# Half of the relu to VectorE, five more gathered columns to ScalarE, one register load for two chunks on SyncE

## The chip, the cores and the metric

One Trainium2 chip, of which the program uses one core. The metric is the device time of the whole program in microseconds. The kernel before takes 3349.78 us (median of 3 runs, 3347.76 to 3354.19). The engines are called as in the profile: PE is TensorE (PEld its weight loads), DVE is VectorE, ACT is ScalarE, POOL is GpSimd, SP is SyncE; a trailing q means the sequencer of that engine.

## The reference

One message-passing layer of a graph network: 12,500 nodes of 48 features, 400,000 edges with 32 features each, sorted by destination.

```python
h   = maximum(layernorm(x), 0)                       # 12500 x 48
tmp = concatenate([h[dst], h[src], edge_attr], 1)    # 400000 x 128
e   = relu(tmp @ W1 + b1)                            # 400000 x 128
msg = e @ W2 + b2                                    # 400000 x 48
out = x + segment_sum(msg, dst, 12500)
```

## The kernel before

The product with `W1` is split by its inputs. Two tables are made once: table A is `h @ W1[:48] + b1` and table B is `h @ W1[48:96]`, both 12,544 rows of 128 floats in the chip's memory; B is also kept transposed in SBUF (`bt`, one column of 128 values for each node). The edges are then taken in 391 chunks of 8 tiles of 128 edges. For a tile, `pre` in PSUM is the sum of a matmul that spreads the few rows of table A that the chunk needs and adds the edge features (`before`, line 409), and of the rows of table B that belong to the tile's source nodes (`gathered`, line 430). `hidden` (line 446) is the relu of the whole chunk out of PSUM, by ScalarE. `fold` (line 456) multiplies by a 0/1 matrix `hot` to sum over equal destinations, `add` (line 471) adds the result into a window `seg` of SBUF, and every 12 to 44 chunks (103 for the first) a full window is multiplied by `W2`, added to x and stored.

Source rows reach a tile in one of three ways, and the tiles are dealt out so that all engines have a share:

- **POOL**: an indirect DMA for each tile, 128 rows of table B into `gb` (line 379). `gb` has 8 buffers, one for each chunk.
- **Columns**: VectorE and ScalarE copy single columns out of `bt` into `gt` (line 352). A register holds the place of each column; `numbers` (line 276) loads a group of registers at once. `PARTS` lists eleven groups for each chunk with their places and sizes: five of VectorE (8, 15, 16, 20, 12: 71 columns) and six of ScalarE (12, 8, 8, 20, 12, 12: 72 columns). 143 columns for each chunk make one whole tile in every 128/143 of a chunk; `BYCOLS` deals these tiles out over chunks 5 to 389.
- **Rows**: SP sends 15 DMAs of one row for each chunk into `gs` (line 293), by registers that it has loaded with the start row of table A (line 369).

The schedule is written by hand (`manual_schedule`): each engine runs its instructions in the order of the program text. In turn `c` of the loop, chunk `c` is prepared (`prepare`: SP loads `lhs`, `row`, the registers and `rhs`, POOL gathers, VectorE makes the 0/1 matrix `lhs` at line 387), chunk `c-1` goes through `before`, `gathered` and `hidden`, and chunk `c-2` through `fold` and `add`. VectorE's order in a turn is `lhs`, columns 8 and 15, `add`, columns 16, `hot` (line 398), columns 20, columns 12. ScalarE's is columns 12, 8, 8, `hidden`, columns 20, 12, 12. PE's is `before`, `fold`, `gathered`. `pre`, `hot` and `p_g` have two buffers, `lhs`, `rhs`, `row` and `hid` three.

Of the kernel before, what the change touches and what calls it, by code (L numbers as in the profile page):

```python
# [8 lines left out]
F32 = mybir.dt.float32  # L9
I32 = mybir.dt.int32  # L10
AF = mybir.ActivationFunctionType
# [5 lines left out]
P = 128  # L17
N, D, DE, HID, E = 12500, 48, 32, 128, 400000
# [4 lines left out]
T = 8  # L23
CE = T * P
NCH = (NT + T - 1) // T
# [29 lines left out]
ROWS0 = 3  # L55
# [2 lines left out]

PARTS = (
    (True, 0, 8), (True, 8, 15), (True, 24, 16), (True, 40, 20), (True, 60, 12),  # L60
    (False, 72, 12), (False, 84, 8), (False, 92, 8), (False, 100, 20), (False, 120, 12),
    (False, 132, 12),
)
PLACE = 23
STRIP = 144
PART = sum(n for _, _, n in PARTS)
SLOT = [at + k for _, at, n in PARTS for k in range(n)]
FIRST_OF = [sum(n for _, _, n in PARTS[:k]) for k in range(len(PARTS))]
RPART = 15
BASE = 0  # L70

BT0 = 16512
SEG0 = 165792
SEG_SIZE = 8 * L


AT_PLACE, AT_SEG, SEG, NEXT = 16, 17, 18, 19
WIDTH = 20
SLOTS = (NCH + 2 + P - 1) // P
BANK = 4  # L80

# [147 lines left out]
def windows(nc, tc, gp, bt, ident, idx, raw, rhss, x_t, tab_a, tab_b, dst, edge_t, w2s, b2s,  # L229
# [5 lines left out]
    with ExitStack() as es:  # L235
# [26 lines left out]
        st = {}  # L262
        gts = {}
        gss = {}

        def group(c):

# [6 lines left out]
        def numbers(c, at, n, engine, table=last):  # L274

            return nc.values_load_multi_w_load_instructions(  # L276
                table[c % P : c % P + 1, c // P, at : at + n],
                engines=[engine], min_val=0, max_val=1 << 23,
                skip_runtime_bounds_check_because="numbers of nodes, and what is made of them",
            )[1]  # L280
# [77 lines left out]
        def prepare(c):  # L358
            n, w = min(T, NT - c * T), span(c)
            at = c * CE  # L360
            lhs = lhss[c % 3]
            nc.sync.dma_start(lhs[W:K, : n * P], edge_t[:, at : at + n * P])
            row = ld.tile([W, CE], I16, name="row")
            nc.sync.dma_start(
                row[:w, : n * P],
                dst[at : at + n * P].rearrange("(o e) -> o e", o=1).to_broadcast([w, n * P]),
            )
            m = max(0, min(RPART, len(BYROWS) * P - (c - ROWS0) * RPART)) if c >= ROWS0 else 0
            base, *nodes = numbers(c, BASE, 1 + m, mybir.EngineType.SP)
            rhs = rhss[c % 3]  # L370
            base = base.with_bounds(min_val=0, max_val=4 * HID * (N - 1))
            nc.sync.dma_start(
                rhs.bitcast(U8)[:w, :],
                taba8[bass.ds(base, 4 * HID * w)].rearrange("(w h) -> w h", w=w),
            )
            st[c] = dict(n=n, rows=nodes)
            gb = gp.tile([P, T, HID], F32, name="gb") if c >= RAW else None
            for t in range(n - len(COLS_OF.get(c, ())) - (c in BYROWS) if c >= RAW else 0):
                nc.gpsimd.indirect_dma_start(  # L379
                    out=gb[:, t, :], out_offset=None, in_=tab_b[:, :],  # L380
                    in_offset=bass.IndirectOffsetOnAxis(
                        ap=srci[:, c * T + t : c * T + t + 1], axis=0
                    ),
                )

            deg = degs[c % 3]
            nc.vector.tensor_scalar(  # L387
                lhs[:w, : n * P], row[:w, : n * P], bw[:w, c : c + 1], None,
                op0=ALU.is_equal, op1=ALU.add, accum_out=deg[:w, :1],
            )  # L390
            st[c].update(rhs=rhs, lhs=lhs, gb=gb, deg=deg)
# [23 lines left out]
        def gathered(c):  # L415

            s = st[c]
            if c < RAW:
                for q in range(T // 2):
                    nc.tensor.matmul(  # L420
                        s["pre"][:, 2 * q : 2 * q + 2, :], s["hx"][:, q, :], wb,
                        start=False, stop=True, skip_group_check=True,
                    )
                return
            pre, js = s["pre"], COLS_OF.get(c, ())
            m = s["n"] - len(js)
            g = m - (c in BYROWS)

            def add(lhsT, rhs, t, e):
                nc.tensor.matmul(  # L430
                    pre[:, t:e, :], lhsT, rhs, start=False, stop=True, skip_group_check=True
                )

            for t, j in enumerate(js, m):
                add(gts.pop(j), ident, t, t + 1)
            if g < m:
                add(ident, gss.pop(c), g, m)
            for t in range(0, g, BANK):
                e = min(g, t + BANK)
                add(ident, s["gb"][:, t:e, :], t, e)  # L440

        def hidden(c):
            s = st[c]
            n = s["n"]
            h = wp.tile([P, T, HID], F32, name="hid")
            nc.scalar.activation(h[:, :n, :], s["pre"][:, :n, :], AF.Relu)  # L446
            s["h"] = h

        def fold(c):
            s = st[c]  # L450
# [61 lines left out]
        with tc.manual_schedule():  # L512
            for c in range(NCH + 2):
                g, k = group(c - 2)
                if c < NCH:
                    prepare(c)
                    rows(c, st[c].pop("rows"))
                if 0 <= c - 1 < NCH:
                    before(c - 1)
                if 0 <= c - 2 < NCH:  # L520
                    fold(c - 2)
                columns(c, 0)
                columns(c, 1)
                segment_add()
                if 0 <= c - 2 < NCH:
                    add(c - 2)
                    if c - 1 == begin(g + 1) < NCH:
                        segment_next(g)
                columns(c, 2)
                if c < NCH:  # L530
                    compare(c)
                if c < 2:
                    nc.vector.memset(segs[c], 0.0)
                columns(c, 3)
                columns(c, 4)
                columns(c, 5)
                columns(c, 6)
                columns(c, 7)
                if 0 <= c - 1 < NCH:
                    gathered(c - 1)  # L540
                    hidden(c - 1)
                columns(c, 8)
                columns(c, 9)
                columns(c, 10)
                if c + 1 == begin(g + 1) or c == NCH - 1:
                    segment_load(g)
                if g > 0 and k < L // BLK:
                    segment_sum(g - 1, k, BLK)
                if g > 0 and k == (STORE if begin(g + 1) < NCH else 2):
                    segment_store(g - 1, L)  # L550
                if c == NCH + 1:
                    segment_sum(g, 0, END_L)
                    segment_add()
                    segment_store(g, END_L)
                if c < RAW:
                    raw_turn(c)
                if c == 1:
                    sources()
                for i in range(c * TURNS, min((c + 1) * TURNS, BLOCKS)):
                    turn(i)  # L560

                if c < PIECES:
                    s = slice(c * PIECE, (c + 1) * PIECE)
                    nc.sync.dma_start(out_t[:, s], x_t[:, s])
# [126 lines left out]
def tile_gnn_preln(  # L691
# [71 lines left out]
    with tc.tile_pool(name="keep", bufs=1) as keep, tc.tile_pool(  # L763
# [82 lines left out]
        def check():  # L846

            p_c = ps_c.tile([1, P], F32, name="p_c")
            nc.tensor.transpose(p_c, furthest, ident)
            out_of = keep.tile([1, 1], F32, name="out_of")  # L850
            nc.vector.tensor_reduce(out_of, p_c, AX.X, ALU.max)
            nc.vector.tensor_scalar(flag, out_of, 0.5, None, op0=ALU.is_gt)

            nc.vector.tensor_scalar(bw, b0f[:W, :], wcol[:W, :], None, op0=ALU.add)

            nc.vector.tensor_scalar(cols, cols, 4, BT0, op0=ALU.mult, op1=ALU.add)
            rows_at = slice(BASE, BASE + 1 + RPART)
            nc.vector.tensor_scalar(
                last[:, :, rows_at], last[:, :, rows_at], 4 * HID, None, op0=ALU.mult
            )  # L860
            nc.vector.tensor_tensor(
                last[:, :, NEXT : NEXT + 1], last[:, :, NEXT : NEXT + 1],
                last[:, :, SEG : SEG + 1], op=ALU.subtract,
            )
            at = last[:, :, AT_PLACE : AT_PLACE + 1]
            nc.vector.scalar_tensor_tensor(
                at, last[:, :, AT_SEG : AT_SEG + 1], -4.0, at, op0=ALU.mult, op1=ALU.add
            )
            at_place = slice(PLACE, PLACE + 1)
            nc.vector.scalar_tensor_tensor(  # L870
                cols[:, :, at_place], cols[:, :, at_place], 1.0, at, op0=ALU.mult, op1=ALU.add
            )
# [87 lines left out]
```

## Time and profile before

| | |
|---|---|
| median of 3 runs | 3349.78 us (3347.76 to 3354.19) |
| the profiled execution | 3348.55 us, of which the span on the core is 3346.8 us |
| granted TensorE clock | 0.875 |
| busy: PE, DVE, ACT, POOL | 84%, 78%, 91%, 75% |
| chunks, and first to last start of the DVE's `lhs` | 391, from 78.3 to 3328.5 us |
| indirect gathers of POOL at line 379 | 2618 |
| column copies of ACT and of DVE | 27705 and 27335 |

Busy time counts an engine's own instructions. Register loads, waits and the issue of DMAs are run by the engine's sequencer and count as idle, so an engine with a busy share of 78% may still have no time left. In a group's row, "idle before" is the idle time in front of its instructions and what ended it; "issue" there is time in which nothing that the profile shows was waited for, only the engine's own sequencer.

### The profile page before, as it was taken

How to read it: one execution, taken by the hardware profiler on the slowest of the kernel's cores; microseconds unless marked ns; L12 is line 12 of the kernel's file. 1: busy time of each engine (PE TensorE's matmuls, PEld its weight loads, DVE VectorE, ACT ScalarE, POOL GpSimd, SP SyncE). 2: the span in 40 equal slices, each digit the busy share in tenths (PEclk: the TensorE clock that was granted, in tenths of full speed). 3: DMA queues.
4: the chain of work that ended last, by engine and by line, in shares of the span. 5: the costliest groups of instructions: out<-in, count | busy, mean ns of one | idle time of the engine just before them, and what ended most of it. 6: DMA issues, size and time to landing. Idle time of an engine off the chain costs nothing.

```text
span 3346.8 us, 114800 instructions
## 1 busy us (share of the span) xinstructions
PE 2804.1 (84%) x16242; PEld 2228.4 (67%) x16242; DVE 2608.9 (78%) x29052; ACT 3044.9 (91%) x28183; POOL 2516.1 (75%) x2672
## 2 busy tenths in 40 slices
PE   7988888888888888888888888888877888788877
PEld 6676767666666676766666676666665666666655
DVE  6477777777777777788777777887878788888886
ACT  5799999999999998999999999999999999999997
POOL 7777777777777777777777777777777777777776
PEclk9988888888888888888888888998989888899898
DMA  7322223233333333333333333333333333333332
GB/s 259 110 77 78 77 77 78 76 80 83 84 83 82 83 82 83 84 89 88 86 86 88 87 88 85 93 91 93 93 93 93 93 90 93 96 100 98 100 98 76
DMA packets 171145, 307.66 MB, mean 92 GB/s; under 512 B 68611, under 2 KB 93813, under 8 KB 169093
## 3 DMA queue, kind: packets, MB, share of 16 engines
q0 software_dynamic: 84800, 172.53, 20.7%
q1 hardware_dynamic: 85170, 127.53, 12.7%
q14 instruction: 634, 5.19, 0.5%
q8 instruction: 137, 2.24, 0.3%
q10 hardware_dynamic: 404, 0.17, 0.0%
HBM read 284.21 MB, written 18.34 MB: 90 GB/s over the span
## 4 chain that ended last, share of the span: by engine, by line
DVE 34%; POOL 25%; issue 22%; PE 10%; ACT 4%; DMA 3%; DVEq 2%; ACTq 0%; SPq 0%; POOLq 0%
POOL gb L379 25%; DVE gt L352 25%; DVE lhs L387 6%; ACT gt L352 3%; DMA gb<-tab_b,srci 3%; PE pre L409 3%; PE pre L430 2%; PE p_g L456 2%; DVE hot L398 2%; DVEq L276 2%; PE p_n L194 1%; ACT hid L446 1%; DVE seg L471 1%; PE pre L306 0%; ACTq L276 0%
## 5 line engine op out<-in xcount | busy, mean ns | idle before, releaser
L379 POOL DMA_INDIRECT gb<-tab_b,srci x2618 | 2476.4, 946 | 805.3 <-issue 759.8
L352 ACT COPY gt<-bt 128x1 f32 x27705 | 2619.5, 188 | 76.6 <-issue 66.1
L352 DVE COPY gt<-bt 128x1 f32 x27335 | 1839.8, 143 | 616.7 <-issue 578.7
L430 PE MATMUL pre<-gb,ident 128*128 128x512 f32 (+2 forms) x1548 | 851.7, 668 | 234.9 <-DMA gb<-tab_b,srci 227.7
L409 PEld LDWEIGHTS pre<-rhs,lhs 112*128 112x128 f32 x6250 | 888.6, 220 | 187.0 <-issue 118.4
L409 PE MATMUL pre<-rhs,lhs 112*128 112x128 f32 x6250 | 884.3, 302 | 27.5 <-issue 17.1
L456 PE MATMUL p_g<-hot,hid 128*128 128x64 f32 (+4 forms) x6250 | 789.9, 279 | 111.2 <-ACT hid L446 109.2
L456 PEld LDWEIGHTS p_g<-hot,hid 128*128 128x128 f32 x6250 | 769.0, 200 | 139.7 <-ACT hid L446 138.8
L430 PEld LDWEIGHTS pre<-gb,ident 128*128 128x128 f32 x1548 | 314.3, 234 | 536.1 <-issue 469.0
L446 ACT ACTIVATE hid<-pre 128x1024 f32<-128x1024 f32 x391 | 397.7, 1017 | 175.4 <-PE pre L430 158.5
L387 DVE TENSOR_SCALAR_CACHE_REDUCE lhs<-row,bw 64x1024 f32<-64x1024 int16 (+4 forms) x391 | 492.2, 1259 | 3.0 <-DMA row<-in_dst 3.0
L430 PE MATMUL pre<-ident,gt 128*128 128x128 f32 x860 | 224.2, 349 | 137.9 <-DVE gt L352 118.8
L430 PEld LDWEIGHTS pre<-ident,gt 128*128 128x128 f32 x860 | 148.6, 217 | 157.6 <-issue 77.6
L398 DVE TENSOR_TENSOR hot<-wnum,rel 128x512 f32<-128x512 f32 (+4 forms) x391 | 207.0, 529 | 0.0
L459 PE MATMUL p_g<-ident,deg 80*128 80x32 f32 (+4 forms) x782 | 159.7, 286 | 0.0
L471 DVE TENSOR_TENSOR seg<-seg,p_g 128x128 f32 (+4 forms) x391 | 94.1, 241 | 80.6 <-PE p_g L459 79.9
L459 PEld LDWEIGHTS p_g<-ident,deg 80*128 80x128 f32 x782 | 128.3, 206 | 0.0
L499 PE MATMUL p_f<-seg,w2s 128*48 128x512 f32 (+1 forms) x58 | 35.9, 705 | 5.5 <-DVE xseg L506 5.1
L773 POOL DMA_INDIRECT xg<-in_x,srci x32 | 31.0, 967 | 10.2 <-issue 8.8
L500 PE MATMUL p_f<-seg,b2s 1*48 1x512 f32 (+1 forms) x58 | 33.3, 656 | 0.0
L203 ACT COPY tab<-p_n 128x512 f32<-128x512 f32 x33 | 18.7, 584 | 12.1 <-PE p_n L194 11.8
L387 DVE DVE_READ_ACCUMULATOR lhs<-row,bw 64x1 f32 (+4 forms) x391 | 28.8, 74 | 0.0
(78 smaller groups left out, 357.7 us busy)
## 6 DMA issues: line engine op xcount, KB each, us to landing
gs<-tab_b SPq DMA_DIRECT2D x5760, 0.5 KB
lhs<-in_edge_t SPq DMA_DIRECT2D x390, 128.0 KB
gb<-tab_b,srci POOLq DMA_INDIRECT x2618
row<-in_dst SPq DMA_DIRECT2D x90, 128.0 KB
row<-in_dst SPq DMA_DIRECT2D x85, 96.0 KB
row<-in_dst SPq DMA_DIRECT2D x50, 160.0 KB
row<-in_dst SPq DMA_DIRECT2D x87, 64.0 KB
tab_b<-tab SPq DMA_DIRECT2D x3, 1280.0 KB
```

What stands on the lines that cost most here:

```text
L276: return nc.values_load_multi_w_load_instructions(table[c % P : c % P + 1, c // P, at : at + n], engines=[engine], min_val=0, max_val=1 << 23,
L352: copy(gts[j][:, e : e + 1], bt8[:, bass.ds(of, 4)].bitcast(F32))
L379: nc.gpsimd.indirect_dma_start(out=gb[:, t, :], out_offset=None, in_=tab_b[:, :], in_offset=bass.IndirectOffsetOnAxis(ap=srci[:, c * T + t ...
L387: nc.vector.tensor_scalar(lhs[:w, : n * P], row[:w, : n * P], bw[:w, c : c + 1], None, op0=ALU.is_equal, op1=ALU.add, accum_out=deg[:w, :1],)
L398: nc.vector.tensor_tensor(hot[:, :n, :], wnum[:, :w].unsqueeze(1).to_broadcast([P, n, w]), rel[:, c * T : c * T + n].unsqueeze(2).to_broad ...
L409: nc.tensor.matmul(pre[:, t, :], s["lhs"][:K, t * P : (t + 1) * P], s["rhs"][:K, :], start=t % BANK == 0, stop=False, skip_group_check=True,)
L430: nc.tensor.matmul(pre[:, t:e, :], lhsT, rhs, start=False, stop=True, skip_group_check=True)
L446: nc.scalar.activation(h[:, :n, :], s["pre"][:, :n, :], AF.Relu)
L456: nc.tensor.matmul(p_g[:, 0, :], s["h"][:, t, :], s["hot"][:, t, :], start=t == 0, stop=t == n - 1)
L459: nc.tensor.matmul(p_g[:, 1, :], s["deg"], ident[:W, :w], start=True, stop=True)
L471: nc.vector.tensor_add(to, to, s["p_g"])
L499: nc.tensor.matmul(p_f[:, :n], w2s, seg[:, 0, s], start=True, stop=False)
```

## The change

- `prepare` loads SP's registers for two chunks in every even chunk: 2 x 15 rows and 2 starts, 32 numbers, in place of 16 in every chunk. The table of numbers is laid out anew for that.
- The relu of a chunk is split. `hidden_first` lets VectorE do tiles 0 to 3 with a `tensor_scalar_max`, and `hidden` leaves tiles 4 to 7 to ScalarE. `gathered` and `hidden_first` stand between VectorE's columns 20 and columns 12; ScalarE's part keeps its place behind its third group.
- ScalarE's groups of columns become 12, 8, 12, 20, 12, 13: 77 columns where there were 72. VectorE's 71 stay. With 148 columns for each chunk, more tiles come from columns and fewer from POOL.

```diff
 PARTS = (
     (True, 0, 8), (True, 8, 15), (True, 24, 16), (True, 40, 20), (True, 60, 12),
-    (False, 72, 12), (False, 84, 8), (False, 92, 8), (False, 100, 20), (False, 120, 12),
-    (False, 132, 12),
+    (False, 72, 12), (False, 84, 8), (False, 92, 12), (False, 104, 20), (False, 124, 12),
+    (False, 136, 13),
 )
+SHARE = 4
-STRIP = 144
+STRIP = 152
 RPART = 15
-BASE = 0
+BASE = 2 * RPART
...
+        ahead = []
...
-            base, *nodes = numbers(c, BASE, 1 + m, mybir.EngineType.SP)
+            if c % 2 == 0:
+                ahead[:] = numbers(c, 0, 2 * RPART + 2, mybir.EngineType.SP)
+            base, nodes = ahead[BASE + c % 2], ahead[c % 2 * RPART :][:m]
...
+        def hidden_first(c):
+
+            s = st[c]
+            s["h"] = wp.tile([P, T, HID], F32, name="hid")
+            nc.vector.tensor_scalar_max(s["h"][:, :SHARE, :], s["pre"][:, :SHARE, :], 0.0)
+
         def hidden(c):
             s = st[c]
-            n = s["n"]
-            h = wp.tile([P, T, HID], F32, name="hid")
-            nc.scalar.activation(h[:, :n, :], s["pre"][:, :n, :], AF.Relu)
-            s["h"] = h
+            of = slice(SHARE, s["n"])
+            nc.scalar.activation(s["h"][:, of, :], s["pre"][:, of, :], AF.Relu)
...
                 columns(c, 3)
+                if 0 <= c - 1 < NCH:
+                    gathered(c - 1)
+                    hidden_first(c - 1)
                 columns(c, 4)
                 columns(c, 5)
                 columns(c, 6)
                 columns(c, 7)
                 if 0 <= c - 1 < NCH:
-                    gathered(c - 1)
                     hidden(c - 1)
...
```

The rest of the diff lays the numbers out for two chunks on the host and moves the constants that go with it.

More of the change, by code (lines that the diff above doesn't have):

```diff
@@ L69 @@
 RPART = 15
-BASE = 0
+BASE = 2 * RPART
 BT0 = 16512
-SEG0 = 165792
+SEG0 = 166176
 SEG_SIZE = 8 * L
-AT_PLACE, AT_SEG, SEG, NEXT = 16, 17, 18, 19
-WIDTH = 20
+AT_PLACE, AT_SEG, SEG, NEXT = 32, 33, 34, 35
+WIDTH = 36
 SLOTS = (NCH + 2 + P - 1) // P
@@ L856, in check @@
             nc.vector.tensor_scalar(cols, cols, 4, BT0, op0=ALU.mult, op1=ALU.add)
-            rows_at = slice(BASE, BASE + 1 + RPART)
+            rows_at = slice(0, BASE + 2)
             nc.vector.tensor_scalar(
@@ L908 @@
     numbers[2 : NCH + 2, AT_PLACE] = SEG0 + of % 2 * SEG_SIZE - BT0
-    numbers[:NCH, BASE] = first
+    bases = np.pad(first, (0, -NCH % 2)).reshape(-1, 2)
+    numbers[: NCH + NCH % 2 : 2, BASE : BASE + 2] = bases
     numbers[:NCH, SEG] = seg
@@ L920 @@
     rows = by_tile[in_rows].reshape(-1)
-    rows = np.pad(rows, (0, -len(rows) % RPART)).reshape(-1, RPART)
-    numbers[ROWS0 : ROWS0 + len(rows), BASE + 1 : BASE + 1 + RPART] = rows
+    by_chunk = np.zeros((NCH + NCH % 2) * RPART, np.int32)
+    by_chunk[ROWS0 * RPART : ROWS0 * RPART + len(rows)] = rows
+    numbers[: NCH + NCH % 2 : 2, : 2 * RPART] = by_chunk.reshape(-1, 2 * RPART)
     last = np.ascontiguousarray(numbers.reshape(SLOTS, P, WIDTH).transpose(1, 0, 2))
```

## The prediction

> **What bounds the kernel now.** I read the busy shares first, then the costliest groups, then for each engine whether anything outside it ever stops it, and last one turn of VectorE in the timeline. From the page, part 1 and part 5:
>
> ```profile
> PE 2804.1 (84%) x16242; PEld 2228.4 (67%) x16242; DVE 2608.9 (78%) x29052; ACT 3044.9 (91%) x28183; POOL 2516.1 (75%) x2672
> ...
> L379 POOL DMA_INDIRECT gb<-tab_b,srci x2618 | 2476.4, 946 | 805.3 <-issue 759.8
> L352 ACT COPY gt<-bt 128x1 f32 x27705 | 2619.5, 188 | 76.6 <-issue 66.1
> L352 DVE COPY gt<-bt 128x1 f32 x27335 | 1839.8, 143 | 616.7 <-issue 578.7
> ```
>
> By busy time ScalarE looks like the bound and VectorE and POOL like engines with room. The idle columns say otherwise: of POOL's 805.3 us idle, 759.8 are its own issue, and of VectorE's 616.7 in front of its copies 578.7 are issue too, the sequencer fetching registers. So both are nearly full. For POOL, the timeline at the beginning, at its one long stop, and at the end:
>
> ```profile
> 52.58 0.94 POOL L379 DMA_INDIRECT gb<-tab_b,srci  x1 [1.77 <-issue]
> 53.83 0.95 POOL L379 DMA_INDIRECT gb<-tab_b,srci  x1 [0.30 <-issue]
> ...
> 128.07 0.94 POOL L379 DMA_INDIRECT gb<-tab_b,srci  x1 [5.88 <-PE pre L430]
> ...
> 3331.58 0.94 POOL L379 DMA_INDIRECT gb<-tab_b,srci  x1 [0.30 <-issue]
> ```
>
> A gather takes 1.25 us from start to start (53.83 - 52.58), and 2618 x 1.25 = 3273 us fill the 3279 us from 52.58 to 3331.58 but for the one stop of 5.88 us. POOL therefore sets today's end. But VectorE stands just behind it. Its waits in the windows 75 to 400, 400 to 1200, 1200 to 3300 and 3300 to the end, and the count of its `lhs` instructions (two records for each chunk) by stretch:
>
> ```profile
> DVE seg L471 <- PE p_g L459: 27.5, 4, 10.5
> ...
> DVE gt L352 <- issue: 169.5, 320, 1.1
> ...
> DVE gt L352 <- issue: 342.9, 789, 1.1
> DVE seg L471 <- PE p_g L459: 41.0, 24, 4.0
> ...
> DVE seg L471 <- PE p_g L459: 11.4, 4, 4.4
> ...
> 400.00:800.00 400.00, 62.58 (x100) 0.86 0.30 78
> 800.00:1200.00 400.00, 62.04 (x98) 0.85 0.32 83
> ...
> 2400.00:2800.00 400.00, 60.95 (x96) 0.90 0.35 92
> 2800.00:3200.00 400.00, 59.84 (x94) 0.90 0.37 98
> ```
>
> Between 400 and 1200 us VectorE waits for no other engine at all; 198 records are 99 chunks in 800 us, 8.08 us for each. There VectorE sets the pace, and POOL, which began early, lives on its eight buffers of lead. Between 2400 and 3200 the pace is 8.42 us (190 records, 95 chunks) and VectorE now and then waits for PE, which waits for POOL. Over the whole stretch from 1200 to 3300 those waits are only 41.0 us. So VectorE could take about 41 us more, 0.1 us for each of 391 chunks, before the end moves.
>
> **The change, part by part.** *Fewer gathers.* Tiles made of columns number 385 x 143 / 128 = 430 today and 385 x 148 / 128 = 445 then (chunks 5 to 389). 15 gathers fewer are 15 x 1.25 = 18.8 us off POOL: 3348.6 - 18.8 = 3329.8 us if POOL still sets the end.
>
> *ScalarE.* One turn of it, and the price of half a relu, from the only ScalarE and VectorE instructions that bring 512 fp32 values out of PSUM into SBUF:
>
> ```profile
> 1502.46 1.01 ACT L446 ACTIVATE hid<-pre 128x1024 f32<-128x1024 f32 x1
> 1503.38 6.77 ACT L352 COPY gt<-bt 128x1 f32 x72
> 1510.05 1.02 ACT L446 ACTIVATE hid<-pre 128x1024 f32<-128x1024 f32 x1
> ...
> L203 ACT COPY tab<-p_n 128x512 f32<-128x512 f32 x33 | 18.7, 584 | 12.1 <-PE p_n L194 11.8 <-ACT ht L181 0.2
> L201 DVE COPY tab<-p_n 128x512 f32<-128x512 f32 x15 | 10.3, 689 | 9.2 <-PE p_n L194 9.1
> ```
>
> The relu goes from 1.02 to about 0.58 us (-0.43); five copies at (6.77 - 0.19) / 71 = 0.093 us add 0.46. ScalarE's turn of 7.59 us becomes 7.62. Two groups also load four numbers more each. The load itself is in
>
> ```profile
> L276 ACTq TENSOR_LOAD <-cols x2309: 536/787/1855, 121.3 to 3327.1; - x193
> L276 SPq TENSOR_LOAD <-last x421: 275/1192/1482, 76.0 to 3330.4; - x141
> ```
>
> where shortest and median differ by 0.25 us, which I take, as an estimate, for four numbers. Copies in front hide it or not, so 0 to 0.5 us: ScalarE's turn is 7.6 to 8.1 us, below the pace of 8.08 or just at it. I take nothing for it.
>
> *SP.* One load of 16 numbers has a median of 1.19 us; one of 32 for two chunks costs between 1.19 (nothing for length) and 2.38 us. So SP gains 0 to 0.6 us for each chunk. Nothing above shows VectorE or POOL waiting for SP's loads in the steady part, and SP's 15 row DMAs stay. Worth nothing in time either way; the long load every other chunk has three buffers of `lhs` and `rhs` to hide behind.
>
> *VectorE.* One turn, in order of time:
>
> ```profile
> 1507.83 1.26 DVE L387 TENSOR_SCALAR_CACHE_REDUCE lhs<-row,bw 48x1024 f32<-48x1024 int16 x1
> 1509.02 0.07 DVE L387 DVE_READ_ACCUMULATOR lhs<-row,bw 48x1 f32 x1
> 1509.02 1.66 DVE L352 COPY gt<-bt 128x1 f32 x23
> 1510.60 0.24 DVE L471 TENSOR_TENSOR seg<-seg,p_g 128x96 f32 x1
> 1511.44 1.06 DVE L352 COPY gt<-bt 128x1 f32 x16 [0.60 <-issue]
> 1512.42 0.55 DVE L398 TENSOR_TENSOR hot<-wnum,rel 128x384 f32<-128x384 f32 x1
> 1513.42 1.31 DVE L352 COPY gt<-bt 128x1 f32 x20 [0.46 <-issue]
> 1514.98 0.82 DVE L352 COPY gt<-bt 128x1 f32 x12 [0.25 <-issue]
> 1515.72 1.26 DVE L387 TENSOR_SCALAR_CACHE_REDUCE lhs<-row,bw 48x1024 f32<-48x1024 int16 x1
> ```
>
> 7.89 us without a wait for another engine. The relu comes between the 20 and the 12 copies. An instruction starts some 0.07 us before its predecessor's record ends (1509.02 against 1507.83 + 1.26), so the relu starts at 1513.42 + 1.31 - 0.08 = 1514.65. At 0.69 us (the row of L201) its successor starts at 1514.65 + 0.69 - 0.07 = 1515.27, where it now starts at 1514.98. The registers are fetched while the relu runs, one instruction later than today (0.06 us), so by 1515.04; the relu hides the whole gap of 0.25 us and costs 0.29 us net. Bounds: 0.60 us if it hides nothing (0.69 less the overlap), and about zero if it ran in 0.4 us. Some gaps of 0.25 us are longer in other turns (issue waits reach 1.1 us), and the relu hides part of these too; I take 0.28.
>
> [...]
>
> *The new wait.* The relu waits for `gathered` of the chunk before, and behind it on VectorE stand 12 copies and the next `lhs`. PE's turn:
>
> ```profile
> 1509.20 2.02 PE L409 MATMUL pre<-rhs,lhs 112*128 112x128 f32 x16
> 1511.12 1.99 PE L456 MATMUL p_g<-hot,hid 128*128 128x48 f32 x16
> 1512.94 0.39 PE L459 MATMUL p_g<-ident,deg 80*128 80x48 f32 x2
> ...
> 1515.94 0.77 PE L430 MATMUL pre<-ident,gt 128*128 128x128 f32 x2 [2.33 <-DVE gt L352]
> 1516.50 1.91 PE L430 MATMUL pre<-gb,ident 128*128 128x512 f32 x2
> ```
>
> PE runs `before` as soon as this turn's `lhs` is made (1509.20 against 1509.09) and ends `gathered` of the same chunk at 1518.41, 2.7 us into VectorE's next turn, whose relu would come 6.8 us into it. So the new wait costs nothing while PE keeps this phase. But `fold` needs both halves of the relu: today ScalarE's ends at 1511.07 and `fold` follows at 1511.12; VectorE's half ends 7.4 us into its turn, 1515.27. `fold` moves 4 us later and ends 2.2 us after that, 9.6 us after the turn's beginning; VectorE's `add` of that chunk stands 2.77 us into the next turn, at about 8.4 + 2.8 = 11.2. 1.6 us are left.
>
> *The sum.* VectorE pays 0.28 x 390 = 109 us; of its 41.0 us of waits for PE all may go; the 27.5 and 11.4 us of the beginning and end stay. 3348.6 + 109 - 41 = 3416.6 us on the profiled execution, which is 1.2 us under the median: 3418 us, 2.0% slower. Check by pace: 8.08 + 0.28 = 8.36 us for each chunk and nothing for changes of window gives 391 x 8.36 = 3269 us from the first `lhs` at 78.3 to 3347, where `lhs` now ends at 3328; thirteen changes of window and the tail come on top. What is late next is not POOL: it would wait for buffers some 68 + 19 = 87 us.
>
> **The rivals.** *POOL stays the bound, faster.* If the relu took no more of VectorE's turn than the gap it covers plus the 0.1 us that VectorE has free, which is a slot of 0.25 + 0.08 + 0.1 = 0.43 us, the 15 gathers saved would set the end: 3330 us. For it: the gap of 0.25 is in every turn seen, other gaps (0.46, 0.60) might shift. Against: 512 fp32 values out of PSUM took 689 ns at L201. [...] 0.08.
>
> *PE's loop closes on VectorE, still slower.* PE's own work is 2804.1 / 391 = 7.2 us for each chunk, and it waits at times for columns or gathers (2.33 us above). From the point where such a wait eats the 1.6 us left before `add`, or makes `gathered` end later than 6.8 us into a turn, VectorE stands still as well. Half of the turns losing 0.3 us are 59 us: 3418 + 59 = 3477 us. 0.19.
>
> *ScalarE becomes the bound.* It decides if both longer loads are exposed and its turn passes 8.36 us, 0.26 us above the 8.1 just found. Another 0.1 us for each chunk would give 3457 us. 0.04. The SP load may do nothing at all; that changes no number.
>
> **How the numbers follow.** The forecast has 0.63 (its own range 3380 to 3450: 0.2 to 0.36 us for each chunk, with 20 to 41 us of waits recovered), the rivals 0.08, 0.19 and 0.04; 0.03 is left for the point where both effects cancel and 0.03 for other things on the slow side. The range runs from 3375 to 3475. Faster by over 0.2% (about what a measurement of this kernel can tell): 0.08; within it: 0.03; slower: 0.89.
>
> **What would show it.** Right: a VectorE relu near 0.69 us with no gap behind it, `lhs` at 8.3 to 8.5 us throughout, VectorE's waits for `p_g` after 1200 us nearly gone, POOL waiting some 87 us for PE at L430, ScalarE's `hid` waiting longer for PE. Wrong: POOL still unbroken to the end, or a relu under 0.45 us (then 3330), or long waits of VectorE at the relu or at `add` (then the second rival).

## The result, and the profile after

The changed kernel takes 3489.62 us (median of 6 runs, 3477.68 to 3504.22) against 3347.87 us for the kernel before (median of 6 runs; its first three had 3349.78): a ratio of 1.042 (95% interval 1.0404 to 1.0436). It is slower, as forecast, but by 142 us and not by 68, and above the stated range of 3375 to 3475 us. The profiled execution took 3490.28 us with a span of 3488.6.

From the page of after, part 1, the chain by engine (part 4), and the groups (part 5):

```profile
PE 2931.7 (84%) x16272; PEld 2356.5 (68%) x16272; DVE 2811.6 (81%) x29443; ACT 3123.1 (90%) x30103; POOL 2502.7 (72%) x2657
...
ACT 36%; DVE 27%; PE 14%; issue 9%; POOL 5%; ACTq 4%; DVEq 3%; DMA 1%; SPq 1%; POOLq 0%
...
L354 ACT COPY gt<-bt 128x1 f32 x29625 | 2853.3, 187 | 222.4 <-issue 189.5
L354 DVE COPY gt<-bt 128x1 f32 x27335 | 1822.6, 143 | 524.1 <-issue 506.7
...
L455 ACT ACTIVATE hid<-pre 128x512 f32<-128x512 f32 x391 | 230.5, 590 | 93.0 <-DVE hid L450 90.5
L450 DVE TENSOR_SCALAR hid<-pre 128x512 f32<-128x512 f32 x391 | 266.4, 681 | 42.4 <-PE pre L434 37.1
...
L479 DVE TENSOR_TENSOR seg<-seg,p_g 128x128 f32 (+4 forms) x391 | 94.4, 242 | 67.4 <-PE p_g L467 65.6
```

And from the page of before the two groups that these are held against and that the prediction doesn't show:

```profile
L446 ACT ACTIVATE hid<-pre 128x1024 f32<-128x1024 f32 x391 | 397.7, 1017 | 175.4 <-PE pre L430 158.5
...
L471 DVE TENSOR_TENSOR seg<-seg,p_g 128x128 f32 (+4 forms) x391 | 94.1, 241 | 80.6 <-PE p_g L459 79.9
```

VectorE's account closes with four of these numbers. (Busy and idle time of any engine add up to the span, so such an account tells where VectorE's time went, and not by itself that VectorE set the pace.) Its busy time rises by 202.7 us (2811.6 - 2608.9); the idle time before its copies, the register gaps, falls by 92.6 (524.1 against 616.7); the new relu waits 42.4 us; and the waits at `add` (its line is 479 here) fall by about 13 (67.4 against 80.6 in the same group before, of which 79.9 for `p_g`). That is +139 us, and the span grew by 141.8. The first two, the relu less what it hides, are +110 us: the forecast had 109. What the forecast had as a gain of 41 us is a loss of 29. That 110 and 109 agree is partly luck. The register gaps behind `add`, summed over the whole trace, grew from 238 to 269 us, because more adds wait: the mean gap is 0.97 us behind the 70 adds that waited, 0.67 behind the others (before: 0.94 behind 25, 0.62 behind the others). These 31 us belong to the waits. The relu itself then costs some 79 us, and the waits with their gaps some 60.

The waits behind it, of the whole trace of after, by the engine that waits:

```profile
PEld p_g L464 <- DVE hid L450: 432.8, 246, 3.8
...
PEld pre L434 <- ACT gt L354: 112.0, 71, 3.5
POOL gb L383 <- PE pre L434: 105.6, 63, 14.3
ACT hid L455 <- DVE hid L450: 90.5, 107, 9.4
...
DVE seg L479 <- PE p_g L467: 65.6, 75, 8.3
DVE hid L450 <- PE pre L434: 37.1, 40, 1.8
```

`fold` on PE waits for VectorE's relu 246 times in 391 chunks. POOL, the bound of before, now waits 105.6 us for its buffers. ScalarE waits 90.5 us for VectorE's half of the relu, a wait that the prediction did not have. Two turns show what else that wait does (ScalarE, timeline of after; then a turn of before in which the relu waits too, for PE):

```profile
1503.44 0.59 ACT L455 ACTIVATE hid<-pre 128x512 f32<-128x512 f32 x1
1504.14 7.38 ACT L354 COPY gt<-bt 128x1 f32 x77
1512.78 0.60 ACT L455 ACTIVATE hid<-pre 128x512 f32<-128x512 f32 x1 [1.26 <-DVE hid L450]
1514.12 3.09 ACT L354 COPY gt<-bt 128x1 f32 x32 [0.74 <-issue]
...
426.92 1.02 ACT L446 ACTIVATE hid<-pre 128x1024 f32<-128x1024 f32 x1 [0.34 <-PE pre L430]
428.26 6.77 ACT L352 COPY gt<-bt 128x1 f32 x72 [0.32 <-issue]
```

The next group of 20 registers is loaded only once the waiting relu has started (the load's record begins at 1512.79 and takes 1.26 us), and the copies come 0.74 us later than the relu ends. Where the relu didn't wait, the load was done in time: 0.1 us lie between the relu's end at 1504.03 and the copies, and none in the turn of before that the prediction shows (`hid` from 1502.46 to 1503.47, the copies from 1503.38). From the start of a relu that waited to the copies it is 1.34 us in after and 1.34 us in before, though the relu of before is 1.02 us long and that of after 0.60. So in such a turn half a relu saves ScalarE nothing.

### The profile page after: what moved, and what is told of

It is laid out like the page before. It is cut to its first block, busy times and chain, and to the rows that moved or that the text cites. A ratio compares the mean times of both kernels' runs of the same rounds, so it can differ in the third digit from the quotient of the medians.

```text
span 3488.6 us, 116781 instructions
## 1 busy us (share of the span) xinstructions
PE 2931.7 (84%) x16272; PEld 2356.5 (68%) x16272; DVE 2811.6 (81%) x29443; ACT 3123.1 (90%) x30103; POOL 2502.7 (72%) x2657
## 4 chain that ended last, share of the span: by engine, by line
ACT 36%; DVE 27%; PE 14%; issue 9%; POOL 5%; ACTq 4%; DVEq 3%; DMA 1%; SPq 1%; POOLq 0%
ACT gt L354 33%; DVE gt L354 17%; POOL gb L383 5%; PE p_g L464 5%; PE pre L434 4%; ACTq L278 4%; DVE lhs L391 4%; DVE hid L450 3%; DVEq L278 3%; ACT hid L455 3%; DVE hot L402 2%; PE pre L413 2%; PE p_n L195 1%; DVE seg L479 1%; PE p_g L467 1%
## 5 line engine op out<-in xcount | busy, mean ns | idle before, releaser
L354 ACT COPY gt<-bt 128x1 f32 x29625 | 2853.3, 187 | 222.4 <-issue 189.5
L354 DVE COPY gt<-bt 128x1 f32 x27335 | 1822.6, 143 | 524.1 <-issue 506.7
L464 PE MATMUL p_g<-hot,hid 128*128 128x64 f32 (+4 forms) x6250 | 894.2, 296 | 428.8 <-DVE hid L450 385.1
L464 PEld LDWEIGHTS p_g<-hot,hid 128*128 128x128 f32 x6250 | 841.7, 214 | 492.2 <-DVE hid L450 432.8
L434 PE MATMUL pre<-gb,ident 128*128 128x512 f32 (+3 forms) x1548 | 873.4, 702 | 0.0
L413 PE MATMUL pre<-rhs,lhs 112*128 112x128 f32 x6250 | 847.6, 294 | 0.6 <-ACT hid L455 0.6
L434 PEld LDWEIGHTS pre<-gb,ident 128*128 128x128 f32 x1548 | 359.9, 257 | 287.2 <-issue 287.2
L434 PE MATMUL pre<-ident,gt 128*128 128x128 f32 x890 | 261.0, 385 | 101.6 <-ACT gt L354 90.2
L455 ACT ACTIVATE hid<-pre 128x512 f32<-128x512 f32 x391 | 230.5, 590 | 93.0 <-DVE hid L450 90.5
L450 DVE TENSOR_SCALAR hid<-pre 128x512 f32<-128x512 f32 x391 | 266.4, 681 | 42.4 <-PE pre L434 37.1
L434 PEld LDWEIGHTS pre<-ident,gt 128*128 128x128 f32 x890 | 176.4, 246 | 118.6 <-ACT gt L354 112.0
L479 DVE TENSOR_TENSOR seg<-seg,p_g 128x128 f32 (+4 forms) x391 | 94.4, 242 | 67.4 <-PE p_g L467 65.6
```

What stands on the lines that cost most here:

```text
L354: copy(gts[j][:, e : e + 1], bt8[:, bass.ds(of, 4)].bitcast(F32))
L413: nc.tensor.matmul(pre[:, t, :], s["lhs"][:K, t * P : (t + 1) * P], s["rhs"][:K, :], start=t % BANK == 0, stop=False, skip_group_check=True,)
L434: nc.tensor.matmul(pre[:, t:e, :], lhsT, rhs, start=False, stop=True, skip_group_check=True)
L450: nc.vector.tensor_scalar_max(s["h"][:, :SHARE, :], s["pre"][:, :SHARE, :], 0.0)
L455: nc.scalar.activation(s["h"][:, of, :], s["pre"][:, of, :], AF.Relu)
L464: nc.tensor.matmul(p_g[:, 0, :], s["h"][:, t, :], s["hot"][:, t, :], start=t == 0, stop=t == n - 1)
```

## The experiments

Theory A: ScalarE's half of the relu waits for VectorE's, and this wait, with the register load behind it, is what costs beyond VectorE's own work. Theory B: ScalarE's 77 copies and longer loads are too much by themselves. Theory C, the second rival of the prediction: the late relu closes a loop, VectorE's relu, `fold` on PE, VectorE's `add`, and VectorE stands still in it. (The expectation of e1 has the way back through `gathered` to the relu. What the traces showed goes through `add` as well, and C stands for both.)

**e1, two tiles for `hid`.**

```diff
-            s["h"] = wp.tile([P, T, HID], F32, name="hid")
+            s["h"] = wp.tile([P, SHARE, HID], F32, name="hid")
...
+            s["k"] = wp.tile([P, T - SHARE, HID], F32, name="hid2")
```

> The whole change, but the two halves of the relu are written into two tiles, so that ScalarE's half need not wait for VectorE's. Theory A (that wait costs the time: ScalarE stands 90.5 us for VectorE's half, and its load of 20 registers, which starts only when the wait is over, adds some 0.5 us to each turn): VectorE sets the pace again at 8.4 us, 3405 to 3435 us. Theory B (ScalarE's own work, 77 copies and longer loads behind a shorter relu, is too long by itself): 3465 to 3495 us. Theory C (the loop VectorE's relu, fold, gathered, VectorE's relu costs the time): 3465 to 3495 us, with VectorE and PE still waiting for each other.

3481.06 us, ratio 1.041 (1.0393 to 1.0427). The edit did not take the wait away. In its trace ScalarE still waits for VectorE's relu:

```profile
ACT hid L456 <- DVE hid L450: 85.4, 104, 5.9
```

So the output tile is not the ground of it. The two halves also read one tile `pre` in PSUM, VectorE its tiles 0 to 3 and ScalarE its tiles 4 to 7. The time lies where B and C had put it, but since the wait is still there, the run neither supports nor refutes A.

**e2, no split; e3, split with 72 columns; e4, the load for two chunks alone.** e2 puts the whole relu back to ScalarE with `gathered` behind the columns, e3 puts back `PARTS`, e4 does both.

> Only the 77 columns and the load for two chunks; ScalarE does the relu of all eight tiles where it did. Theory A: ScalarE's turn grows from 7.9 by 0.46 us for five copies and up to 0.1 for loads, to 8.35 to 8.45: 3390 to 3430 us. Theory B: ScalarE is the bound and its two longer loads are exposed, 8.6 us or more: over 3450 us. If ScalarE had room for five columns: 3330 us.

> The split of the relu in one tile and the load for two chunks, but 72 columns as before. Theory A: ScalarE's turn loses 0.55 us and its wait for VectorE remains, so VectorE's 8.4 us set the pace, with the loop still felt: 3415 to 3450 us. Theory B: ScalarE is relieved, 3415 us. Theory C: nothing changes, 3475 to 3495 us.

> Only the load of 32 numbers for two chunks on SP; all else as before. All theories: 3343 to 3353 us, no change, since nobody waits for SP's loads. If the long load every other chunk delayed lhs or rhs, 3360 us or more.

| | median us | ratio to before (95%) |
|---|---|---|
| e4: load for two chunks | 3348.46 | 1.0008 (0.9999 to 1.0018) |
| e2: that and 77 columns | 3408.86 | 1.0190 (1.0173 to 1.0207) |
| e3: that and the split | 3470.71 | 1.0372 (1.0345 to 1.0399) |
| the whole change | 3489.62 | 1.0420 (1.0404 to 1.0436) |

e4 came out as expected. e2 lies in the range that stood under A, 3390 to 3430 us, which is ScalarE's turn with five more copies, and below B's 3450. e3 lies above A's and B's ranges and 4 us under C's. The load for two chunks is worth nothing. Five columns alone cost 64 us: ScalarE becomes the bound. The chain of e2 says so, and ScalarE's `hid`, which waited 158.5 us for PE before, now waits 18.2:

```profile
ACT 71%; PE 11%; DVE 7%; ACTq 6%; issue 4%; DVEq 1%; DMA 0%; POOL 0%; SPq 0%
...
ACT hid L456 <- PE pre L434: 18.2, 27, 3.5
```

The split alone costs 125 us; the columns add only 19 on top of it, probably because ScalarE, relieved of half the relu, is then not far beyond the pace that VectorE sets. ScalarE as the bound is therefore true of the columns alone, and not the cause of most of the loss. Nor is A in e3. ScalarE's relu waits there for VectorE's even longer than in the whole change, but the chain of work that ended last hardly goes through ScalarE (ACT 4% of it before, 5% in e3):

```profile
DVE 34%; POOL 25%; issue 22%; PE 10%; ACT 4%; DMA 3%; DVEq 2%; ACTq 0%; SPq 0%; POOLq 0%
...
DVE 54%; PE 15%; issue 13%; POOL 6%; ACT 5%; DVEq 4%; DMA 1%; ACTq 1%; SPq 0%; POOLq 0%
...
ACT hid L455 <- DVE hid L450: 213.1, 252, 7.4
```

In the whole change ScalarE has 36% of the chain, so its wait may have a part in the last 19 us.

For C, the timelines of e3 in one bad turn, PE and then VectorE, and the granted clock there (the column in front of the DMA share):

```profile
1519.38 3.65 PE L464 MATMUL p_g<-hot,hid 128*128 128x48 f32 x16 [2.47 <-DVE hid L450]
1522.83 0.63 PE L467 MATMUL p_g<-ident,deg 80*128 80x48 f32 x2
...
1518.64 0.68 DVE L450 TENSOR_SCALAR hid<-pre 128x512 f32<-128x512 f32 x1
1519.24 0.81 DVE L354 COPY gt<-bt 128x1 f32 x12
...
1523.49 0.26 DVE L479 TENSOR_TENSOR seg<-seg,p_g 128x96 f32 x1 [0.86 <-PE p_g L467]
1524.71 0.40 DVE L354 COPY gt<-bt 128x1 f32 x5 [0.96 <-issue]
...
1514.00:1519.00 5.00, 2.90 (x20) 2.21 (x18) 3.73 (x46) 5.00 (x56) 3.77 (x4) 0.99 0.28 73
1519.00:1523.50 4.50, 4.12 (x19) 4.12 (x20) 3.64 (x39) 3.61 (x35) 3.43 (x4) 0.50 0.34 92
```

The relu ends at 1519.32 and `fold` starts at 1519.38. At a granted clock of 0.50 it takes 3.65 us where the prediction's row has 1.99 at a clock of 1.00 (before, 1510 to 1515 us), and with the two matmuls of the degrees ends 4.1 us after the relu. `add` stands still for 0.86 us, and the register gap behind it is 0.96 us where it was 0.60. The prediction left 1.6 us for such things; in this turn 1.1 us are there (from the relu's end to 1522.63, where the copies before `add` end, less the 2.2 us of `fold` at full clock), and half the clock takes 1.9. Before, the same `fold` ended 4.9 us ahead of its `add` (1505.74 against 1510.60), so the clock could fall unnoticed. The turn is typical: over the whole trace of e3, `fold` and the degrees took 3.5 us on average, at a mean granted clock of 0.64, ahead of the 85 adds that waited, and 2.3 us at 0.96 ahead of the other 305.

**e5 and e6: `pre` in two tiles as well.** e5 is the whole change with `pre` and `hid` each in two tiles, e6 the same with 72 columns. **e7 and e8** are e5 and e6 with the relu ahead of `hot`:

```diff
-            pre = ps_p.tile([P, T, HID], F32, name="pre")
+            pre = [ps_p.tile([P, BANK, HID], F32, name=f"pre{k}") for k in range(2)]
...
                 columns(c, 2)
+                if 0 <= c - 1 < NCH:
+                    gathered(c - 1)
+                    hidden_first(c - 1)
```

> The whole change with pre and hid each in two tiles, one for each half, so that neither half's relu names a tile of the other's. (13 copies of the setting up become 26, some 10 us.) Theory A, now with the shared PSUM tile as the ground of the wait: ScalarE's wait for VectorE's relu (85 to 90 us before) is gone and both engines turn at 8.4 us: 3410 to 3445 us. Theory B (ScalarE too long by itself, over 8.6 us): 3455 us or more. Theory C (the loop through fold, whoever waits for whom): 3460 to 3490 us.

> The same with two tiles each and 72 columns: the split of the relu and the load for two chunks alone, without the wait. Theory A: VectorE's 8.4 us for each chunk are all that is left, 3405 to 3435 us. Theory B: ScalarE relieved by 0.5 us, 3405 to 3435 us as well. Theory C: 3455 to 3475 us, as with one tile.

> Two tiles each, 77 columns, and VectorE's relu stands before hot, ahead of the load of 20 registers with its gap of 0.46 to 0.73 us, instead of ahead of the load of 12 with 0.25. Theory A: the relu is hidden but for 0.0 to 0.3 us, VectorE turns at 8.2 to 8.3, ScalarE at 8.2 to 8.4: 3345 to 3410 us. Theory B: ScalarE alone sets 8.6 us, 3455 us or more. Theory C: fold comes 2 us earlier and the loop loosens, 3400 to 3430 us.

> As the last with 72 columns. Theory A: VectorE at 8.2 to 8.3 us, ScalarE under 8.1, POOL's gathers as before: 3345 to 3380 us. Theory B: the same. Theory C: 3390 us or more.

These and all later runs came to chips on which the kernel before itself took 5390 to 5511 us, so their times can only be held against before on the same chip, and not against the numbers that were expected. In the traces taken there the copies come slowly for stretches, here ScalarE's in e10, one in 0.72 us, where the 22 copies from 1502.80 on took 2.14 us, one in 0.093:

```profile
1505.88 0.19 ACT L354 COPY gt<-bt 128x1 f32 x1 [0.53 <-issue]
1506.59 0.19 ACT L354 COPY gt<-bt 128x1 f32 x1 [0.51 <-issue]
1507.32 0.19 ACT L354 COPY gt<-bt 128x1 f32 x1 [0.55 <-issue]
```

Why, no run shows. The same kernels were run again, and again on such chips:

> [...] The whole change with pre and hid each in two tiles. Theory A (VectorE's 8.4 us are left): 3410 to 3445 us. Theory B (ScalarE over 8.6 us): 3455 us or more. Theory C (the loop through fold): 3460 to 3490 us.

> The same kernel as e6, once more. Two tiles each and 72 columns. Theories A and B: 3405 to 3435 us. Theory C: 3455 to 3475 us.

> The same kernel as e7, once more. Two tiles each, 77 columns, VectorE's relu before hot. Theory A: 3345 to 3410 us. Theory B: 3455 us or more. Theory C: 3400 to 3430 us.

> The same kernel as e8, once more. Two tiles each, 72 columns, VectorE's relu before hot. Theories A and B: 3345 to 3380 us. Theory C: 3390 us or more.

> The same kernel as e5 a third time, in the hope of a chip on which the kernel before takes some 3345 us. The whole change with pre and hid each in two tiles. Theory A (VectorE's 8.4 us are left): 3410 to 3445 us. Theory B (ScalarE over 8.6 us): 3455 us or more. Theory C (the loop through fold): 3460 to 3490 us.

> The same kernel as e6 a third time. Two tiles each, 72 columns. Theories A and B: 3405 to 3435 us. Theory C: 3455 to 3475 us.

> The same kernel as e8 a third time. Two tiles each, 72 columns, VectorE's relu ahead of hot. Theories A and B: 3345 to 3380 us. Theory C: between 3345 us, if the loop had been all, and 3390 us or more.

> The same kernel as e6 once more: two tiles each, 72 columns. Where the kernel before takes some 3345 us: 3405 to 3435 us by theories A and B, 3455 to 3475 us by theory C. Where it takes some 5400 us: 2 to 2.6% longer than before, as in the three runs so far, which would tell nothing new.

**e9 and e10: one tile each, 72 columns.** e9 has the relu ahead of `hot`; e10 leaves the relu and moves `add` behind `hot`:

```diff
-                if 0 <= c - 2 < NCH:
-                    add(c - 2)
...
                 columns(c, 2)
                 if c < NCH:
                     compare(c)
+                if 0 <= c - 2 < NCH:
+                    add(c - 2)
```

> The split in one tile, 72 columns, load for two chunks, with VectorE's relu before hot instead of behind the 20 copies; to be held against e3 (3471 us). Theory A (ScalarE's wait for VectorE is what costs): the wait stays, 3430 us or more. Theory C (the loop): relu and fold come some 2 us earlier, add has slack again, and the gap before the 20 copies (0.58 us) hides the relu better than that before the 12 (0.38): VectorE's own turn 8.2 to 8.3, POOL near its bound, 3350 to 3390 us.

> The split in one tile, 72 columns, load for two chunks, relu where the change has it, but VectorE's add stands behind hot, 1.9 us later; to be held against e3 (3471 us). Theory A: no change, 3460 us or more. Theory C: the waits of VectorE at add (0.155 us for each chunk) and the longer register gaps behind them go, 3395 to 3430 us, which is VectorE's own turn alone.

| on chips where before takes 5390 to 5511 us | ratio to before (95%), run by run |
|---|---|
| e5: two tiles, 77 columns | 1.0184 (1.0157 to 1.0211), 1.0189 (1.0163 to 1.0215), 1.0267 (1.0237 to 1.0298) |
| e6: two tiles, 72 columns | 1.0200 (1.0172 to 1.0228), 1.0206 (1.0180 to 1.0232), 1.0262 (1.0231 to 1.0293), 1.0191 (1.0164 to 1.0217) |
| e7: e5, relu ahead of `hot` | 0.9968 (0.9955 to 0.9981), 0.9983 (0.9971 to 0.9995) |
| e8: e6, relu ahead of `hot` | 0.9784 (0.9761 to 0.9808), 0.9781 (0.9756 to 0.9807), 0.9801 (0.9772 to 0.9829) |
| e9: one tile, 72 columns, relu ahead of `hot` | 0.9857 (0.9841 to 0.9874) |
| e10: one tile, 72 columns, `add` late | 0.9886 (0.9870 to 0.9903) |

VectorE's waits for `fold` at `add` in e6 (last run), in e8 (last run) and in e10, and ScalarE's wait for VectorE's relu in e9 and in e10:

```profile
DVE seg L481 <- PE p_g L469: 154.1, 166, 8.2
...
DVE seg L481 <- PE p_g L469: 24.8, 6, 8.0
...
DVE seg L479 <- PE p_g L467: 4.0, 2, 2.3
...
ACT hid L455 <- DVE hid L450: 176.7, 196, 5.2
...
ACT hid L455 <- DVE hid L450: 165.9, 175, 5.1
```

What follows, for these chips: with the wait of ScalarE gone (in e5, too, `hid` of ScalarE waits for PE and not for VectorE) but the relu late, the split still costs 1.8 to 2.7%. With the wait in place but `add` moved out of the loop (e10), or the relu moved ahead (e9), it costs nothing, and the kernel is 1.1% and 1.4% faster than before, in one run of each on one chip. e6 and e8 differ only in the place of the relu, and on the three chips that ran both, 4.2 to 4.6 points lie between their ratios. So the place of the relu against `add` decides here, and not the wait alone: this is C. e10 and e6 differ in the tiles too, so that the 3% between them is not a clean measure of `add` alone.

A rival is left: ahead of `hot` the relu also stands ahead of the load of 20 registers, and may hide a longer gap than ahead of the 12 (0.46 against 0.25 us in the turn of before that the prediction shows). VectorE's rows speak against it as the main part. From e6 to e8 on the first of the three chips, where the span falls by 238 us, VectorE's idle time at `add` falls by 181 us (213.7 to 32.8) and that before its copies by 77 (2147.9 to 2070.7); on the other two it is 180 and 72 of 248 us, and 241 and 25 of 255.

Two things stay open. None of e5 to e10 was measured on a chip where before takes 3345 us; there C rests on the traces of e3 and of the change. And neither e3 nor the whole change was run on the other chips. Taken as ratios, e5 and e6 lie about where A had put them (1.018 to 1.030 of before) and below C's 1.033 to 1.043, so the shared tile may cost something there, too; what A and C each take is not known. Why e8 to e10 are faster than before, no run shows: before was not traced on those chips.

## Why the prediction was right or wrong, point by point

- **The bound.** It fits what came: with VectorE longer, POOL waits for buffers, 105.6 us at line 434's `pre` where 87 were forecast (some of it is 0.3 us of ordinary issue put down to that line). What it left out is that ScalarE was as full (below).
- **VectorE's relu.** Right in length: 681 ns against 689 from the row of line 201's copy, and no gap behind it in an undisturbed turn. The 110 us net over the kernel against 109 are partly luck: 31 of them are longer gaps behind `add`, and the relu itself cost some 79, less than forecast. The first rival, POOL as the bound at 3330 us, falls.
- **"Of its 41.0 us of waits for PE all may go."** Wrong, and this is the step that failed: the forecast let the old waits go and put the new ones at nothing. Its check of slack (1.6 us between `fold` and `add`) was made with `fold` at full clock. It was also too large by its own rows: from the relu's end at 1515.27 it is 0.74 us of copies and 2.77 us of the next turn to `add`, 3.5 us less the 2.2 of `fold` and the degrees, so 1.3 us; the 1.6 come from counting the turn as 8.4 us, of which the rows fill only 8.2. Between 400 and 1200 us, where before has no wait, VectorE now waits at the relu and at `add`, and from 1200 to 3300 the two together are as long as the 41.0 us of before:

```profile
DVE hid L450 <- PE pre L434: 9.5, 10, 1.7
DVE seg L479 <- PE p_g L467: 6.8, 16, 0.8
...
DVE hid L450 <- PE pre L434: 23.6, 24, 1.8
DVE seg L479 <- PE p_g L467: 20.7, 42, 0.9
```

  The old waits came from POOL's late gathers and did go (before, then after):

```profile
PEld pre L430 <- DMA gb<-tab_b,srci: 65.8, 52, 4.0
...
PEld pre L434 <- DMA gb<-tab_b,srci: 3.8, 8, 0.5
```

  New ones took their place, which belong to the loop. The term was -41 us and should have been +29, or some +60 with the longer gaps behind `add`.
- **The second rival** named this: a wait that eats the 1.6 us before `add`, or a `gathered` that ends after the relu's place, 3477 us. It had 0.19 and came true in kind; its size is 13 us short of the 3490. The trace of before already had 63 of 390 `fold`s at a mean clock below 0.99 and 21 that took over 3.0 us with the degrees, which should have been set against the slack. But it would not have given the size: in after it is 137 and 94.
- **ScalarE, "I take nothing for it."** Wrong twice, though only some 19 us of the loss hang on the columns beside the split. Five columns by themselves cost 64 us (e2), since ScalarE had no more room than VectorE. And the split added a wait for VectorE, 90.5 us, with `pre` in one PSUM tile (85.4 in e1 with `hid` in two tiles; in e5, with `pre` in two as well, ScalarE's `hid` waits for PE), which the prediction's list of waits lacked: it looked only at what PE and VectorE wait for. In the whole change ScalarE's busy time rises by 78 us and the idle time before its copies by 146 (222.4 against 76.6), while its idle time before `hid` falls by 82 (93.0 against 175.4): +142 us as well. By these rows it is as full as VectorE.
- **SP.** Right: 1.0008 (e4). The long load takes some 2.1 us at the median, and the time doesn't change.
- **Marks given beforehand.** VectorE's waits for `p_g` after 1200 us nearly gone: not met, up to 3300 us they are halved, 20.7 us against 41.0. VectorE's `lhs` at 8.3 to 8.5 us throughout: not met. It is 372 records, 186 chunks, in the two stretches below, 8.6 us each:

```profile
400.00:800.00 400.00, 59.24 (x93) 0.80 0.29 75
800.00:1200.00 400.00, 58.50 (x94) 0.81 0.31 80
2400.00:2800.00 400.00, 58.57 (x93) 0.85 0.34 91
2800.00:3200.00 400.00, 58.38 (x92) 0.86 0.36 93
```

  ScalarE's `hid` waiting longer for PE: not met, it waits for VectorE. The granted clock is also lower than before in the same stretches (0.80 and 0.81 against 0.86 and 0.85), and `fold` is longer at a lower clock (3.65 us at 0.50 above); what lowers the clock the runs don't show. The sign of being wrong that was named, waits of VectorE at the relu or at `add`, did come.

## What to carry to other kernels

When half of a step moves to an engine that does it later in its turn, count who consumes the result, and how far that consumer's own product then lies ahead of the next reader; and take that slack at the lowest clock that the trace grants (0.50 in the turn of e3 above), not at the full one. Waits that an engine has today because another one is late are not a reserve that a longer turn may use: if the longer turn brings the engine into a loop with the other, new waits come in their place. The same work placed two instructions earlier was worth 4% and more of the time (e6 against e8, on the chips with the longer times). And an account of one engine that closes does not name the engine that sets the pace: here VectorE's and ScalarE's both close.

## What the runs showed of the hardware

- In the trace of after a register load behind a relu of ScalarE that waited started only when the wait was over: its record begins at 1512.79 us behind the relu that waited until 1512.78, and the gap is 0.74 us there, about 0.1 us behind the relu at 1503.44 that didn't wait. Behind VectorE's `add` it is 0.96 us after a wait of 0.86 (e3), 0.60 without (before). These short waits were so made longer by a load that was hidden, in whole or in part, where nothing waited.
- ScalarE's register loads in the trace of after take 0.56 us at the median for 8 numbers, 0.80 for 12, 1.04 for 13 and 1.28 for 20: the thirteenth number took 0.24 us more, as much as the four from 8 to 12 (0.24).
- On five chips the kernel before took 5390 to 5511 us instead of 3345 us, at a granted clock near 0.70; in the traces of the other kernels taken there copies come one in 0.72 us for stretches.
- Where VectorE reads tiles 0 to 3 of one PSUM tile `pre` and ScalarE tiles 4 to 7, ScalarE waits for VectorE (85.4 us in e1 with two output tiles); with two PSUM tiles ScalarE's `hid` waits for PE instead (85.2 us in the third run of e5).
